# A graph layer on one Trainium2 core: more groups sorted by source, and a first product in one 16-bit pass

## The chip, the cores and the metric

The kernel runs on one core of a Trainium2 chip. Its engines are TensorE (PE, with its weight loads as PEld), VectorE (DVE), ScalarE (ACT), GpSimd (POOL) and SyncE (SP), which mostly issues DMAs. The metric is the device time of one execution in microseconds; times of one kernel agree within about 0.3%.

## What is computed

The reference is one layer of a graph network with residuals, on 6250 nodes of 128 features and 100,000 edges with 4 attributes each. The edges come sorted by their destination. In short:

```python
msg_in = concatenate([x[src], x[dst], edge_attr], axis=1)      # 100000 x 260
h = silu(msg_in @ mW1 + mb1)                                   # 100000 x 128
messages = h @ mW2 + mb2
aggregated = segment_sum(messages, dst, num_segments=6250)
u = silu(concatenate([x, aggregated], axis=1) @ uW1 + ub1)
y = layer_norm(x + (u @ uW2 + ub2), ln_g, ln_b)
out = layernorm(x + y)
```

All inputs and outputs are 32-bit floats. The first product is linear, so it splits into `x[src] @ Wa + x[dst] @ Wb + edge_attr @ We`; the kernel makes two tables, `tab_a = x @ Wa` and `tab_b = x @ Wb + mb1`, once per node.

## The kernel before

Edges are worked through in 98 groups of 1024 (8 tiles of 128). As they are sorted by destination, a group touches few destination nodes: a window of W = 80, which begins at the group's first destination (`base`).

**An unsorted group** (82 of the 98) takes these steps. GpSimd gathers a row of `tab_a` for every edge, with one indirect DMA per tile (`fetch`, L229). SP loads the destinations, broadcast to 80 partitions (`near`, L430), the 80 rows of `tab_b` (`mv`, L584) and the attributes (`st`, L585). VectorE makes two one-hot matrices: `st`, node by edge, with a sum along it that gives the degrees (L593), and `oh`, edge by node (L603). TensorE then multiplies `st` by `mv` (`before_rows`, L618): a 32-bit product per tile with 84 rows, 80 nodes and 4 attributes, into a PSUM buffer `pre`, of which there are two. VectorE adds the gathered rows (L645) and ScalarE applies silu (L646). TensorE sums the result by destination with `oh`, 8 products of 112 columns into the single buffer `pt` (`sums`, L648), and VectorE adds that to `acc`, at an offset in a window of 768 nodes (`add`, L689). The degrees of four groups are transposed and added together (`count`, L679). The first five groups gather rows of `x` instead (`RAW`) and multiply them by Wa on TensorE.

**A sorted group** (16: every fifth from group 15) gathers nothing. Its edges are put in order of their source; then the rows of `tab_a`, which lie in SBUF in three 16-bit parts, are selected by one-hot matrices `O`: per group 168 products of 16 bit into the buffer `po` (`select`, L1051). ScalarE and VectorE make `O` (`picks`, L1016); `Oc` and `at_s` bring the attributes into the new order (`attribute_part`, L1034); `st_s` and `mv_s` give the part of the destinations (L1044). The hidden rows are transposed back (`turned_hidden`, L1072), summed and added as in other groups. These steps are spread over six stages, the group's distance `d` from 5 to 0 (`sorted_before`, `sorted_behind`).

The sort itself is a bitonic network on VectorE (`sort_steps`, L820), over 128 partitions that hold 128 edges each, eight partitions to a group. It runs in steps beside the tables and the first eight groups.

**Order.** The instructions' order on each engine is written by hand (L1179 to 1231). A stage belongs to one unsorted group g: SP loads for the group three stages ahead (`LEAD`), VectorE makes the matrices of the one two ahead, `before_rows` and `hidden` are those of the next, then come the sorted group's parts, then the sums of g and the work on finished nodes (`node_stage`, in batches of 512 nodes). Table b is made batch by batch: two batches ahead of the groups, the others in the stages (`make_b`, L457; `x_stage(k) + 2`). Gathers are paced: every other one waits for a product that a count of TensorE's work chooses (L1242 to 1258). A buffer that is still in use makes the engine wait that would write it, and the queue behind it.

Before all that the tables are built (`tables`, L1136), with the lists of destinations (`lists_1` to `lists_3`). A second way through the kernel, `general`, is only taken for inputs whose destinations are spread too far; it is not taken here.

Of the kernel before, what the change touches and what calls it, by code (L numbers as in the profile page):

```python
# [21 lines left out]
P = 128  # L22
# [5 lines left out]
def kernel(  # L28
# [28 lines left out]
    W = 80  # L57
    WS = 112
    NW = NP + W
    AW = 768  # L60
    K1 = W + ED
# [24 lines left out]
    Q0, QD, QN = 15, 5, 16  # L86
    by_sort = {Q0 + QD * q: q for q in range(QN)}
    listed = [g for g in range(NG) if g not in by_sort]
    R = QN * G
# [6 lines left out]
    assert R % 32 == 0 and W <= S0 and S0 + G * ED == P and listed[RAW] == RAW  # L96
# [10 lines left out]
    def made_for(g):  # L107
        stage = stage_of(g - 4) - 1 if g in by_sort else turn_of(g) - LEAD
        return max(k for k in range(NB) if k < 2 or x_stage(k) + 2 < stage)
# [98 lines left out]
    w_row_i = first.tile([P, W], I32, name="w_row_i")  # L208
    nc.gpsimd.iota(w_row_i, pattern=[[1, W]], base=0, channel_multiplier=0)
# [13 lines left out]
    tab_b = dram.tile([NW, H], F32, name="tab_b")  # L223
    sd = dram.tile([4, QN * GE], F16, name="sd")
    ea_d = dram.tile([ED, NG * GE], F32, name="ea_d")
# [3 lines left out]
    def fetch(g):  # L229
# [20 lines left out]
        ceil_i, pattern=[[BN * P, NB + 1], [0, G]], base=BN * P - W, channel_multiplier=0  # L250
    )
    pos_i = first.tile([R, P], I32, name="pos_i")
    nc.gpsimd.iota(pos_i, pattern=[[P, P]], base=0, channel_multiplier=P * P)
# [8 lines left out]
    if rest:  # L262
        nc.vector.memset(dst_l[low:NG], N)
    nc.sync.dma_start(dst_l[:low], dst[: low * GE].rearrange("(p j) -> p j", j=GE))
# [8 lines left out]
    dst_l = dst_l[:NG]  # L273
    w_row = ps1.tile([P, W], F32, name="w_row")
# [17 lines left out]
    deg_s = []  # L292
    for k in range(3):
        deg_s.append(consts.tile([W, P], F32, name=f"deg_s{k}"))
        nc.vector.memset(deg_s[k], 0.0)

    def deg_at(g):
        s, i = divmod(g - 1, 4) if g else (-1, 0)
        return deg_s[(s + 1) % 3], 32 * i

    def deg_col(g):
        t, c = deg_at(g)
        return t[:, c : c + 1]
# [19 lines left out]
    def lists_1():  # L323
        base_c = first.tile([NG, 1], F32, name="base_c")
        nc.vector.tensor_copy(base_c, dst_l[:, 0:1])
        rel_n = first.tile([P, GE], F32, name="rel_n")[:NG]
        nc.vector.tensor_scalar(rel_n, dst_l, base_c, None, op0=OP.subtract)
        parts.update(base_c=base_c, rel_n=rel_n)
        nc.vector.memset(floor_i[:, 0:1], 0)
        nc.vector.memset(floor_i[:, last[NB - 2] + 1 :], batches[NB - 1][0] * P)  # L330
        nc.vector.memset(ceil_i[:, 84 + G // 2 :], batches[NB - 1][0] * P - W)
# [98 lines left out]
    def destinations(g):  # L430
        near[g] = work.tile([P, GE], I32, name="near")[:W]
        n = min(GE, E - g * GE)
        if n < GE:
            nc.vector.memset(near[g][:, n:], N)
# [1085 lines left out]
```

## Time and profile before

| | |
|---|---|
| median of three runs | 1079.45 us (1077.62 to 1081.79) |
| the profiled execution | 1078.25 us, span of its instructions 1076.5 us |
| mean granted TensorE clock | 0.863 of full speed; in the records it is 1.0 or 0.5 |
| gathers on GpSimd | 614 from `tab_a` (mean 980 ns), 40 from `x` (959 ns) |
| `st` and `oh` on VectorE | 82 at 1261 ns, 82 at 816 ns |
| `O` on ScalarE | 128 at 711 ns and 64 at 1148 ns |
| loads of `near`, `mv`, `st` | 320, 40 and 16 KB per unsorted group |
| DMA | 108.94 MB in 86,890 packets, mean 101 GB/s |

A line of groups reads: line of the kernel, engine, operation, what is written from what, with the shapes, and how often; then the busy time in us and the mean ns of one; then the idle time of the engine just before these instructions, and what ended most of it ("issue" is a wait for nothing that the profile shows). In a timeline the first two numbers are the start and the duration in us of a run of like instructions. The records of TensorE overlap, since products are pipelined: what one costs is read from start to start. A 32-bit product has two records, a 16-bit one has one. In a table of stretches each engine has its busy us and its instructions; PEclk is the granted clock.

### The profile page before, as it was taken

To read this page: it belongs to the slowest core of one execution; us is meant where nothing else is said; L and a number is where in the kernel's file an instruction comes from. 1 tells how busy PE (TensorE), PEld (TensorE's weight loads), DVE (VectorE), ACT (ScalarE), POOL (GpSimd) and SP (SyncE) were. 2 spreads that over 40 slices of the span, in tenths; PEclk is the share of its full clock that TensorE was granted. 3 is DMA by queue.
4 is the path that set the end of the run, shared out by engine and by line. 5 is a ranking of instruction groups with operands and counts; after the bars stand their busy time and mean duration, and the time that the engine had idled before them with its cause. 6 is when DMAs were issued, how large, how long until landed. Compare 5 with 4: busy or idle time off the path is not lost.

```text
span 1076.5 us, 17905 instructions
## 1 busy us (share of the span) xinstructions
PE 807.8 (75%) x6479; PEld 687.8 (64%) x6479; DVE 558.1 (52%) x1357; ACT 404.1 (38%) x543; POOL 641.9 (60%) x665
## 2 busy tenths in 40 slices
PE   5548557668878788877877878777878877877874
PEld 4548455566757576666776666666577666676653
DVE  3463677843555283555373555444374445473282
ACT  1122114533343354344344353343253344363142
POOL 6646557765656666565666566556566566666550
PEclk8778779789888989798998989879879788999795
DMA  9544315342424252525163443424343434242220
GB/s 231 140 114 117 93 57 143 87 101 81 114 85 116 72 137 76 121 75 131 57 152 84 117 109 97 110 80 100 87 112 93 99 92 120 71 111 81 85 77 25
DMA packets 86890, 108.94 MB, mean 101 GB/s; under 512 B 22348, under 2 KB 63456, under 8 KB 86794
## 3 DMA queue, kind: packets, MB, share of 16 engines
q1 hardware_dynamic: 52498, 58.26, 21.3%
q0 software_dynamic: 20928, 42.90, 15.2%
q10 hardware_dynamic: 13368, 6.56, 2.3%
q8 instruction: 53, 0.87, 0.4%
q14 instruction: 43, 0.35, 0.1%
HBM read 96.26 MB, written 11.40 MB: 100 GB/s over the span
## 4 chain that ended last, share of the span: by engine, by line
PE 52%; issue 16%; DVE 13%; another core or an unknown queue 7%; ACT 5%; DMA 3%; POOL 2%; SPq 1%; DVEq 0%; ACTq 0%; POOLq 0%
PE pt L148 14%; PE po L148 14%; PE pre L148 13%; PE pn L148 8%; PE pn L151 2%; POOL ga L234 2%; DMA ga<-tab_a,src_i 1%; DVE st L593 1%; DVE oh L603 1%; ACT h L646 1%; DVE ga L645 1%; ACT O L1027 1%; PE pre L151 1%; DVE O L1023 1%
## 5 line engine op out<-in xcount | busy, mean ns | idle before, releaser
L234 POOL DMA_INDIRECT ga<-tab_a,src_i x614 | 601.9, 980 | 380.4 <-issue 202.4
L148 PE MATMUL pre<-mv,st 128*128 128x128 f32 x1308 | 202.3, 310 | 27.4 <-issue 12.8
L148 PEld LDWEIGHTS pre<-mv,st 128*128 128x128 f32 x1308 | 190.5, 225 | 40.3 <-issue 29.2
L148 PE MATMUL pt<-oh,h 128*128 128x112 f32 x1308 | 191.5, 305 | 25.6 <-issue 12.6
L148 PEld LDWEIGHTS pt<-oh,h 128*128 128x128 f32 x1308 | 180.1, 218 | 39.5 <-issue 24.3
L646 ACT ACTIVATE h<-ga 128x1024 f32<-128x1024 f32 (+1 forms) x78 | 81.1, 1042 | 317.7 <-DVE ga L645 222.6
L692 DVE TENSOR_TENSOR acc<-acc,pt 128x80 f32 x98 | 23.3, 238 | 341.3 <-PE pt L148 104.1
L148 PE MATMUL po<-O,A_low 128*128 128x157 bf16 (+47 forms) x896 | 163.8, 225 | 22.3 <-issue 22.3
L148 PE MATMUL po<-O,A 128*128 128x156 bf16 (+37 forms) x1376 | 140.2, 227 | 36.6 <-issue 33.0
L148 PEld LDWEIGHTS <-A 128*128 128x128 bf16 x1376 | 112.4, 104 | 58.3 <-issue 57.3
L645 DVE TENSOR_TENSOR ga<-ga,pre 128x1024 f32<-128x1024 f32 (+1 forms) x78 | 93.3, 1197 | 54.7 <-PE po L148 22.0
L593 DVE TENSOR_SCALAR_CACHE_REDUCE st<-near,base_p 80x1024 f32<-80x1024 int32 x82 | 103.4, 1261 | 11.9 <-issue 10.4
L148 PEld LDWEIGHTS <-A_low 128*128 128x128 bf16 x896 | 91.0, 103 | 20.6 <-issue 20.3
L1027 ACT ACTIVATE O<-sc,p_less 128x512 bf16<-128x512 f16 x128 | 84.8, 711 | 1.4 <-DMA sc<-sd 1.4
L1028 ACT ACTIVATE O<-O,ones 128x1024 bf16<-128x1024 bf16 x64 | 73.5, 1148 | 2.1
L603 DVE TENSOR_TENSOR oh<-w_row,rel 128x640 f32<-128x640 f32 x82 | 66.9, 816 | 0.8
L151 PE MATMUL pn<-ident,hT 128*128 128x128 f32 x128 | 23.2, 310 | 45.1 <-issue 10.2
L1070 ACT ACTIVATE hT<-po 128x512 f32<-128x512 f32 x32 | 19.0, 593 | 91.4 <-PE po L148 51.7
L234 POOL DMA_INDIRECT ga<-in_x_dram,src_i x40 | 38.3, 959 | 23.2 <-issue 9.9
L151 PEld LDWEIGHTS pn<-ident,hT 128*128 128x128 f32 x128 | 15.5, 154 | 51.1 <-issue 24.3
L148 PE MATMUL pt<-oh,h_s 128*128 128x112 f32 x256 | 34.8, 290 | 12.6 <-ACT h_s L1079 7.9
L148 PE MATMUL pn<-Oc,at_s 128*128 128x512 f32 x64 | 37.8, 675 | 8.0 <-issue 5.6
(221 smaller groups left out, 921.9 us busy)
## 6 DMA issues: line engine op xcount, KB each, us to landing
near<-in_dst_dram SPq DMA_DIRECT2D x81, 320.0 KB
ga<-tab_a,src_i POOLq DMA_INDIRECT x614
sc<-sd SPq DMA_DIRECT2D x16, 512.0 KB
mv<-tab_b SPq DMA_DIRECT2D x82, 40.0 KB
tab_a<-A SPq DMA_DIRECT2D x11, 256.0 KB
tab_b<-o SPq DMA_DIRECT2D x11, 256.0 KB
out_dram<-o ACTq DMA_DIRECT2D x11, 256.0 KB
x<-in_x_dram SPq DMA_DIRECT2D x10, 256.0 KB
```

The lines of the kernel that those rows point to most:

```text
L148: counted(nc.tensor.matmul(to, *operands, **flags), to, share)
L151: counted(nc.tensor.transpose(to, *operands), to)
L234: ins = nc.gpsimd.indirect_dma_start(out=rows[g][:, i, :], out_offset=None, in_=x if g < RAW else tab_a[:, :], in_offset=bass.IndirectOffs ...
L593: nc.vector.tensor_scalar(stbuf[turn_of(g) % NST][:W], near.pop(g), base_p[:W, g : g + 1], 0.0, op0=OP.is_equal, op1=OP.add, accum_out=deg ...
L603: nc.vector.tensor_tensor(oh[g][:, :n, :W], w_row[:, None, :].to_broadcast([P, n, W]), rel[:, g, :n, None].to_broadcast([P, n, W]), op=OP. ...
L645: nc.vector.tensor_add(s[:, i], s[:, i], p[:, i])
L646: nc.scalar.activation(h[:, i], s[:, i], AF.Silu)
L692: nc.vector.tensor_add(to, to, pt[:, :W])
L1023: nc.vector.tensor_scalar(O[:, j], key, p_rows[:, r : r + 1], None, op0=OP.is_equal)
L1027: nc.scalar.activation(O[:, j], key, AF.Square, bias=p_less[:, r : r + 1])
L1028: nc.scalar.activation(O[:, 2:], O[:, 2:], AF.Relu, bias=ones[:, 0:1], scale=-1.0)
L1070: nc.scalar.activation(now["hT", half], now.pop("po"), AF.Silu)
```

## The change

Two things change together, and several follow from them.

1. **More sorted groups.** Every fourth group from 15 on is sorted, 20 instead of 16. In the sort 80 partitions hold 256 edges each, four to a group.
2. **The first product in one 16-bit pass.** The table b and We are split into three 16-bit parts each (high, middle, low), the attributes too. The product of a tile has 126 rows: 3 parts x 30 nodes, and 9 pairs of parts x 4 attributes. The 30 nodes move with the tile: tile i of a group begins 8 i nodes behind the group's base. The base is a multiple of 8, and a new margin F = 16 lies ahead of table b and the sums.

What follows: the split table is kept in DRAM by eighths (`tab_p`), and a group's `mv` takes four DMAs; `near` comes from a stored 16-bit table of offsets (`off_d`), 90 partitions of 2 KB; the attributes come as 36 rows of 2 KB. `st` is one comparison of 16-bit values without a sum. `oh` has 32 columns per tile, padded to 112. The sums go to overlapping columns of `pt`, so the buffer is first cleared by a product with zeros, and the degrees are made by four products with ones. A group's window has W = 88 nodes. The splits of table b and of the attributes are made in steps spread over a stage (`b_steps`, `attribute_steps`), in a `pre` buffer.

The diff, cut to its core:

```diff
+    S = 8
+    V, VS, VW = 30, 32, 112
+    W = S * (G - 1) + VS
+    F = 2 * S
+    KB, K1 = 3 * V, 3 * V + 9 * ED
-    Q0, QD, QN = 15, 5, 16
+    Q0, QD, QN = 15, 4, 20
+    GR = 4
+    C = GE // GR
...
     def destinations(g):
-        near[g] = work.tile([P, GE], I32, name="near")[:W]
...
-            dst[g * GE : g * GE + n].rearrange("(o e) -> o e", o=1).to_broadcast([W, n]),
+        near[g] = work.tile([P, GE], F16, name="near")[:KB]
+        nc.sync.dma_start(near[g], off_d[g : g + 1, :].to_broadcast([KB, GE]))
...
+    def attribute_steps(c, pm):
...
+        def high():
+            nc.scalar.copy(v, ea_l.pop(c).rearrange("q (j d) -> q d j", d=ED))
+            nc.scalar.copy(t[:, 0], v)
+
+        def middle():
+            nc.vector.tensor_sub(v, v, t[:, 0])
+            nc.scalar.copy(t[:, 1], v)
+
+        def low():
+            nc.vector.tensor_sub(t[:, 2], v, t[:, 1])
+            nc.scalar.dma_start(
...
+    def b_steps(k, pm):
...
+        def high():
+            nc.vector.tensor_add(v, v, b1[:m, None, :].to_broadcast([m, BN, H]))
+            nc.scalar.copy(t[:, :, 0], v)
+            tb = node.tile([P, BN, H], F32, name="o")[:m]
+            nc.scalar.copy(tb, v)
...
+        def middle():
+            nc.vector.tensor_sub(v, v, t[:, :, 0])
+            nc.scalar.copy(t[:, :, 1], v)
+
+        def low():
+            nc.vector.tensor_sub(t[:, :, 2], v, t[:, :, 1])
...
-        nc.sync.dma_start(mv[turn_of(g) % NM][:W], tab_b[bass.ds(bases[g], W), :])
-        nc.sync.dma_start(stbuf[turn_of(g) % NST][W:K1], ea_d[:, g * GE : (g + 1) * GE])
+        to = mv[turn_of(g) % NM].rearrange("r i f -> r (i f)")
+        for a in range(D - G + 1):
+            n = min(S, V - a * S)
+            nc.sync.dma_start(
+                to[3 * S * a : 3 * S * a + 3 * n],
+                tab_p[:n, :, bass.ds(bases[g] + a, G), :].rearrange("b s d f -> (b s) (d f)"),
+            )
+        cols = slice(g * GE, (g + 1) * GE)
+        nc.sync.dma_start(
+            stbuf[turn_of(g) % NST][KB:K1],
+            ea_d[:, cols].rearrange("(o r) e -> o r e", o=1).to_broadcast([3, 3 * ED, GE]),
+        )
...
         nc.vector.tensor_scalar(
-            stbuf[turn_of(g) % NST][:W],
-            near.pop(g),
-            base_p[:W, g : g + 1],
-            0.0,
-            op0=OP.is_equal,
-            op1=OP.add,
-            accum_out=deg_col(g),
+            stbuf[turn_of(g) % NST][:KB], near.pop(g), third[:KB], None, op0=OP.is_equal
         )
...
             matmul(
-                pre[g][:, i, :], st[:, i, :], mv[turn_of(g) % NM], start=True, stop=not raw
+                pre[g][:, i, :], st[:K1, i, :], mv[turn_of(g) % NM][:K1, i, :],
+                start=True, stop=not raw, share=1 / 4,
             )
...
+    def cleared(pt):
+        matmul(pt, none[:, : pt.shape[0]], none, start=True, stop=False, share=1 / 4)
+
+    def degrees(g, pt):
+        to = pt[0:1, WP : WP + W]
+        if g in by_sort:
+            transpose(to, deg_s[by_sort[g] % 2], ident[:W, :W])
+            return to
+        for a in range(D - G + 1):
+            matmul(
+                to[:, a * S : (a + G) * S], ones[:, 0:1], oh[g][:, :, a * S : (a + 1) * S],
...
+            cleared(pt)
+            if g < NG - 1:
+                degrees(g, pt)
+            for i in range(n):
+                matmul(
+                    pt[:, i * S : i * S + VW], h[:, i, :], oh[g][:, i, :],
+                    start=False, stop=i == n - 1,
+                )
...
+        chain = []
+        for k in range(2, NB):
+            if j == x_stage(k) + 2:
+                chain = b_steps(k, wide()[:, :BN])
         for c in range(1, NC):
-            at = stage_of(max(1, c * EC // GE - 9))
+            at = stage_of(max(1, c * EC // GE - 10))
...
+                chain = [None] + attribute_steps(c, wide().rearrange("p i f -> p (i f)"))
+        chain = iter(chain)
+
+        def go_on():
+            step = next(chain, None)
+            if step:
+                step()
```

`go_on` is called four times in a stage: at its start, after the matrices, after the silu of the next group, and after the sums.

## The prediction

> **What bounds the kernel now.** I read the page's first part and the busy times by stretch, then the groups, the chain of waits, and the timelines of TensorE and GpSimd.
>
> ```profile
> PE 807.8 (75%) x6479; PEld 687.8 (64%) x6479; DVE 558.1 (52%) x1357; ACT 404.1 (38%) x543; POOL 641.9 (60%) x665
> ```
> ```profile
> core 0: us, PE busy (x) PEld busy (x) DVE busy (x) ACT busy (x) POOL busy (x), PEclk, DMA share, GB/s
> 0.00:89.00 89.00, 51.88 (x288) 46.93 (x289) 37.74 (x131) 17.16 (x23) 53.23 (x65) 0.79 0.60 157
> 89.00:239.00 150.00, 101.87 (x738) 90.18 (x736) 100.05 (x253) 47.18 (x52) 97.03 (x92) 0.82 0.37 99
> 239.00:1039.00 800.00, 632.16 (x5357) 534.59 (x5358) 405.23 (x918) 325.57 (x443) 486.02 (x503) 0.89 0.39 99
> 1039.00:1076.00 37.00, 21.86 (x102) 16.06 (x100) 15.05 (x55) 14.17 (x26) 5.65 (x6) 0.68 0.11 31
> ```
>
> The stretch 239 to 1039 is the steady part. TensorE is busy 79% of it. GpSimd's 503 gathers look like 61%, but its timeline shows the real load:
>
> ```profile
> 454.74 0.95 POOL L234 DMA_INDIRECT ga<-tab_a,src_i  x1 [0.49 <-issue]
> 455.99 0.95 POOL L234 DMA_INDIRECT ga<-tab_a,src_i  x1 [0.30 <-issue]
> 457.25 0.94 POOL L234 DMA_INDIRECT ga<-tab_a,src_i  x1 [0.31 <-issue]
> ```
>
> A gather costs 1.25 us from start to start, 10.0 us for a group of 8; 503 of them fill 629 of 800 us, also 79%. The two are level, and tied both ways: gathers are paced by products, and a group's products need its gathered rows. VectorE (51%) and ScalarE (41%) have room. The chain through this stretch is mostly TensorE ("po" 18.1%, "pt" 15.9%, "pre" 11.8%, "pn" 10.3%) and "issue" 17.4%; 9.6% of it, 77 us, is an unknown queue (5.2%), gathers (2.6%) and their landing (1.8%). So TensorE binds, and gathers bind in places. The groups show the holes:
>
> ```profile
> L148 PE MATMUL pre<-mv,st 128*128 128x128 f32 x1308 | 202.3, 310 | 27.4 <-issue 12.8
> L148 PEld LDWEIGHTS pre<-mv,st 128*128 128x128 f32 x1308 | 190.5, 225 | 40.3 <-issue 29.2
> L148 PEld LDWEIGHTS <-A 128*128 128x128 bf16 x1376 | 112.4, 104 | 58.3 <-issue 57.3
> ```
>
> The last column is idle time with no visible cause: 57.3 us before 1376 16-bit loads, about 42 ns each.
>
> **The change, part by part.** Busy means overlap, so TensorE is costed from start to start, at full clock:
>
> ```profile
> 307.55 1.95 PE L148 MATMUL pre<-mv,st 128*128 128x128 f32 x16
> 309.33 1.02 PE L148 MATMUL po<-st_s,mv_s 128*128 128x512 f32 x2
> ```
> ```profile
> 326.73 0.27 PE L148 MATMUL po<-O,A 128*128 128x130 bf16 x2
> 326.84 0.22 PE L148 MATMUL po<-O,A_low 128*128 128x130 bf16 x1
> 326.90 0.28 PE L148 MATMUL po<-O,A 128*128 128x125 bf16 x2
> ```
>
> Sixteen 32-bit records of "pre" (two per product) take 1.78 us, 0.222 per product. Two 16-bit products of 130 columns take 0.11 us, 0.055 each.
>
> *First product.* 654 products by 0.222 (145.2 us) become 622 by 0.055 (34.2): -111.0 us. Here I weigh the Trainium skill, "TensorE: Matmul & The Clock Gate", section "Back-to-back issue gap": it puts a sustained 128-column load-and-multiply pair at about 81 ns. By it the term is 622 x 0.026 = 16 us less good, which would cancel the whole TensorE gain below. The row is the same pair on this chip; I take 0.055.
>
> *Degrees.* VectorE no longer sums them; each unsorted group gets a clearing product of 256 columns (16-bit; by the row, 256/130 x 0.055 = 0.11) and four 32-bit products of 64 columns with one stationary column. Half of "pre" is 0.056 per record; two records, four products: 0.45. Over 78 groups +44 us, less 26 transposes (-4), plus 20 for sorted groups (+2). The four may run as low as the load allows (0.2 us) or as high as a 128-column product (0.9): 25 to 79 us.
>
> *Four more sorted groups.* Beyond the sums that every group has, one costs TensorE about 9 us of selection (168 products at a mean of some 0.054 in the timeline), four records of "pn<-Oc" (0.435 each, 1.74), four of "po<-st_s" (0.43, 1.72) and 8 transposes (0.115, 0.9): 13.4 us, times 4 = +53.5.
>
> TensorE's sum: -111 + 44 - 2 + 53.5 = -15.5, divided by the page's mean granted clock 0.863: **-18 us**. In steady groups it is no gain: with sums of 1.8 us per group and 3.5 us of node work per five groups, five before take 4 x 3.6 + 15.2 + 3.5 = 33 us at full clock (6.6 each), four after 3 x 2.85 + 15.2 + 2.8 = 26.6 (6.6 each). Freed time is respent on sorting.
>
> *Gathers.* 32 fewer, 32 x 1.25 = 40 us of GpSimd. Per group the floor falls from 8.0 to 7.5 us; in a cycle of three unsorted groups and a sorted one it is 30 us, against about 40 that TensorE with its holes needs (before 40 of 51). Of the 77 us that gathers hold on the chain I let 30 go: that is between 0, if those waits are the landing latency that stays, and 60. **-30 us.** What is late next there is TensorE.
>
> *VectorE.* Per unsorted group L593 (1261 ns plus 78 for the read) becomes a 16-bit comparison without sum: twice the row "O<-sc" 128x512 bf16 (0.36), so 0.65; L603 goes from 640 to 256 elements, 0.82 to 0.42. Saved 1.1 us x 78 = 86. Added: two subtractions per batch of table b (13 x 1.4), as many per attribute chunk (10 x 1.2), four sorted groups (4 x 7, rows L1005 to L1085). It lies beside TensorE; I count 0. The sort has 104 compare operations of 128 elements where it had 98 of 64 at about 0.2 us; at 0.27 to 0.30 it is 8 to 11 us longer. It runs between groups 0 and 8 and was on the chain at 141 to 147 us; these groups save 8 x 1.1 on the same engine. Sum 0. Without that cover, +10.
>
> *ScalarE.* +12.6 us per sorted group (8 x 0.711, 4 x 1.148, hT and h_s 4 x 0.58) = +50, and three copies of 0.6 per batch: 404 becomes about 490, 46%. Hidden.
>
> *The chains of splits.* Table b and the attribute chunks are now split in four steps through one stage, in one of the two "pre" buffers. The last subtraction (0.69 us, as L462) stands on VectorE behind acc (0.24) and deg (0.23) of the same stage; the next stage's first product waits for that buffer, and behind it on TensorE the sorted products and the sums. So up to 1.4 us in 20 stages: 0 to 28, where node products stand between it is covered; I take **+8**.
>
> *Tables.* Steps written inline make VectorE wait for ScalarE: for two batches 2.7 us each, for chunk 0 about 2. The stretch to 69 us has VectorE idle 57%, but TensorE waits for its copies (L468). SP gets 23 more small DMAs (filling we_d, off_d and tab_p; 0.3 to 0.4 us each) and holds behind them tab_a's writes. 0 to 16; **+8**.
>
> *Queues in the steady part.* SP issues 6 DMAs for an unsorted group instead of 3 (four for mv), some 25 per cycle at 0.3 to 0.45: 10 of 40 us. A write of tab_p waits for loads of mv under way, and later loads for it (L463 did so 7 times, 19.6 us); behind it stand near, mv and st, with a lead of two stages, 20 us. Moved per group: (3 x 432 + 800) / 4 = 524 KB against 459, gathers 384 against 410: +4% at a DMA share of 0.39. Nothing charged. The skill speaks against one load: "DMA: Bandwidth & Descriptors", section "Rules for kernel authors", says that a leading dimension of c under 16 confines a DMA to c engines. The attribute load now leads with 3: 72 KB on 3 engines, 24 KB each, about 0.9 us at the page's 27 GiB/s, against 4 KB on 4. The trace has no such transfer; with three stages of lead I take 0, and by the rule, if gathers wait for those three engines, 78 x 0.9 = 70 us of their time is at stake, little of it on the chain.
>
> *Issue holes.* Hardware instructions on TensorE, counted in both built programs (four per 32-bit product, two per 16-bit), rise from 12,960 to 14,520. If holes go with time, 0. If with pairs, 672 more selections by about 36 ns (98 us over 2688 in the three groups of A) are +24, the first product -7, the degrees +14: +31. I take **+6**, nearer to time, since the holes come in clusters and not evenly.
>
> Sum: -18 - 30 + 8 + 8 + 6 = -26 on the profiled execution's 1078.25 us (span 1076.5): 1052. The median of the runs is 1.2 higher, 1079.45: **1053.5 us**.
>
> **The rivals.** *Holes go with instructions (slower).* TensorE is the only bound, gathers give back nothing, and the issue holes before 16-bit loads grow with the denser stream: -18 + 8 + 8 + 31 = +29, 1108 us. For it: per steady group TensorE's work is not smaller. Against it: 77 us of gathers on the chain. It decides as soon as the holes cost more than what the gathers give back, about 30 us.
>
> *Gathers were the bound.* Then the 40 us and half of what else they hold go: -60 with -18 and +16: 1017 us. For it: 79% forced load. Against it: TensorE rarely waits for gathered rows directly.
>
> *Give and take.* Relief, holes and chains cancel: 1079, within 5 us. That the change does not do what it says is excluded: the built program has one 16-bit pass per tile and 20 sorted groups.
>
> **How the numbers follow.** Forecast 40% (own range 1028 to 1073), gathers 12%, cancelling 8%, holes 40% (1085 to 1125). A measurement of this kernel tells 0.5% (5.4 us) from no change. Faster 0.50, same 0.09, slower 0.41. As both signs hold weight, the range spans them: 1012 to 1115.
>
> **What would show it.** "pre" as 16-bit with one record per tile, 8 of them in about 0.45 us; degrees near 0.45 us a group; 622 gathers at the same 1.25 us; the unknown and gather shares of the steady chain falling from 77 us to under 50; "issue" idle before 16-bit loads near 42 ns each (if it grows, the slower rival holds). TensorE waiting for a VectorE subtraction before "pre" for more than 1.4 us a time would show the chains mis-sized. The forecast is wrong if a cycle of four groups takes over 41 us between 239 and the last sorted group.

## The result, and the profile after

The changed kernel takes 1109.95 us, the median of four runs (1107.92 to 1115.91). The kernel before, run on the same chip, takes 1080.62 us (1077.62 to 1083.15). The ratio is 1.028 with an interval of 1.023 to 1.033: the change makes the kernel slower by 29 us. The profiled execution took 1110.15 us, its span is 1108.4 us, and the mean granted clock is 0.847 (before 0.863). Executions of one kernel differ by more than the 0.3% given above: by 0.7% here, and by up to 2.2% in the runs below.

These are the busy times of the engines, and then the table by stretch, with the same bounds as before except for the end.

```profile
PE 845.2 (76%) x7234; PEld 685.3 (62%) x7234; DVE 509.8 (46%) x1370; ACT 474.2 (43%) x662; POOL 618.9 (56%) x635
```
```profile
0.00:89.00 89.00, 44.93 (x207) 39.71 (x208) 37.44 (x128) 18.34 (x28) 45.42 (x59) 0.90 0.59 153
89.00:239.00 150.00, 101.68 (x736) 82.88 (x736) 91.90 (x250) 53.40 (x63) 96.62 (x93) 0.75 0.44 118
239.00:1039.00 800.00, 652.33 (x5971) 528.20 (x5970) 351.09 (x892) 378.56 (x533) 453.01 (x460) 0.86 0.42 106
1039.00:1108.00 69.00, 46.28 (x323) 34.49 (x322) 29.41 (x101) 23.92 (x39) 23.84 (x25) 0.79 0.22 59
```

In the steady stretch TensorE is busier than before (652 us for 632), its clock is lower (0.86 for 0.89), and GpSimd does 460 operations in place of 503. VectorE has lost 54 us and ScalarE has gained 53. The groups and the timeline of TensorE show the parts of the change:

```profile
L245 POOL DMA_INDIRECT ga<-tab_a,src_i x582 | 578.7, 994 | 427.4 <-issue 197.9
L158 PEld LDWEIGHTS <-A 128*128 128x128 bf16 x1720 | 145.2, 107 | 89.4 <-issue 89.0
L158 PE MATMUL pre<-mv,st 126*128 126x128 bf16 x622 | 68.1, 254 | 25.5 <-issue 16.5
L158 PE MATMUL pt<-oh,ones 128*1 128x64 f32 x616 | 52.2, 230 | 8.0 <-issue 7.8
```
```profile
628.76 0.28 PE L158 MATMUL pt<-none 1*128 1x256 bf16 x1
628.97 0.61 PE L158 MATMUL pt<-oh,ones 128*1 128x64 f32 x8
629.51 1.70 PE L158 MATMUL pt<-oh,h 128*128 128x112 f32 x13
```
```profile
622.34 0.61 PE L158 MATMUL pre<-mv,st 126*128 126x128 bf16 x8
622.79 0.20 PE L158 MATMUL po<-O,A 128*128 128x19 bf16 x2
```

The first product is one 16-bit record per tile: eight of them take 0.45 us from start to start (622.34 to 622.79), 0.056 each. From start to start the clearing product costs 0.21 us (628.76 to 628.97) and the degrees of a group 0.54 us (628.97 to 629.51).

**Where the time came from.** VectorE adds every group's sums to `acc`, and the start of that addition dates the group. These are group 0's additions, first of the kernel before, then after:

```profile
89.34 0.24 DVE L692 TENSOR_TENSOR acc<-acc,pt 128x80 f32 x1 [10.41 <-PE pt L148]
```
```profile
103.53 0.24 DVE L814 TENSOR_TENSOR acc<-acc,pt 128x88 f32 x1 [6.77 <-PE pre L158]
```

So 14.2 us are lost before group 0. From group 0 to 20 the changed kernel gains 4.9 us (209.3 for 214.2). From group 20 to 92 it takes 747.2 us in place of 722.7: 24.5 us are lost, and a cycle of four groups takes 41.5 us, over the 41 us that the prediction named as its sign of being wrong. The last groups and the end give 2 us back. Together that is 31.9 us, the difference of the spans.

**What TensorE's time consists of.** I took its timeline between 239 and 1039 us apart. A run of like products is charged from its start to the next start, less the idle time in between; what of it lies in stretches of half clock is halved, and the other half is called clock. By the groups whose addition to `acc` falls in the stretch, in us per group:

| kernel | work at full clock | clock | idle | sum | issue idle in 100 us | gathers in 100 us |
|---|---|---|---|---|---|---|
| before | 6.93 | 0.99 | 2.04 | 9.96 | 11.6 | 62.9 |
| after | 7.27 | 1.22 | 1.90 | 10.39 | 8.6 | 57.4 |

"Issue idle" is the part of TensorE's idle time that ends with no cause that the profile shows. So the work rose by 0.34, the lower clock cost 0.23, and the idle time fell by 0.14. The work can be relied on; the other two are no larger than what single profiles of equal steady parts differ by (the table of the next section has e_iota and e_start, which change only the start: 7.32 and 7.31 of work, but 1.04 and 1.00 of clock, where after has 1.22). By the same count, from before to after: first product 1.49 to 0.37, degrees and clearing 0 to 0.59, selection 1.85 to 2.37, the other sorted parts (`pn<-Oc`, `po<-st_s`, `pn<-ident,hT`) 0.86 to 1.18.

### The profile page after: what moved, and what is told of

Same layout as the page of the kernel before. It is cut to its first block, busy times and chain, and to the rows that moved or that the text cites. A ratio compares the mean times of both kernels' runs of the same rounds, so it can differ in the third digit from the quotient of the medians.

```text
span 1108.4 us, 20413 instructions
## 1 busy us (share of the span) xinstructions
PE 845.2 (76%) x7234; PEld 685.3 (62%) x7234; DVE 509.8 (46%) x1370; ACT 474.2 (43%) x662; POOL 618.9 (56%) x635
## 2 busy tenths in 40 slices
DMA packets 115693, 120.04 MB, mean 108 GB/s; under 512 B 50083, under 2 KB 79355, under 8 KB 115583
## 4 chain that ended last, share of the span: by engine, by line
PE 49%; issue 11%; DVE 11%; ACT 8%; another core or an unknown queue 3%; DMA 3%; SPq 1%; ACTq 1%; DVEq 0%; POOL 0%; POOLq 0%
PE pt L158 18%; PE po L158 17%; PE pn L158 7%; PE pre L158 4%; ACT O L1167 2%; DMA ar<-sd 2%; PE pn L161 2%; ACT O L1168 2%; DVE ga L747 1%; DVE st_s L1179 1%; DVE y L871 1%; ACT h L748 1%; ACT o L884 1%; DVE O L1163 1%
## 5 line engine op out<-in xcount | busy, mean ns | idle before, releaser
L158 PE MATMUL po<-O,A 128*128 128x147 bf16 (+37 forms) x1720 | 179.5, 232 | 70.1 <-ACT O L1168 33.2
L158 PE MATMUL po<-O,A_low 128*128 128x144 bf16 (+25 forms) x1120 | 211.5, 230 | 10.7 <-issue 10.5
L158 PEld LDWEIGHTS <-A 128*128 128x128 bf16 x1720 | 145.2, 107 | 89.4 <-issue 89.0
L748 ACT ACTIVATE h<-ga 128x1024 f32<-128x1024 f32 (+1 forms) x74 | 76.7, 1039 | 111.7 <-DMA ga<-tab_a,src_i 48.6
L158 PEld LDWEIGHTS <-A_low 128*128 128x128 bf16 x1120 | 117.3, 106 | 11.2 <-issue 11.2
L158 PE MATMUL pre<-mv,st 126*128 126x128 bf16 x622 | 68.1, 254 | 25.5 <-issue 16.5
L158 PEld LDWEIGHTS <-st 126*128 126x128 bf16 x622 | 54.9, 118 | 34.0 <-issue 30.9
L158 PE MATMUL pt<-oh,ones 128*1 128x64 f32 x616 | 52.2, 230 | 8.0 <-issue 7.8
L158 PE MATMUL pre<-w,xT 128*128 128x128 f32 (+2 forms) x186 | 44.8, 410 | 16.8 <-ACT xT L490 9.1
L158 PE MATMUL pt<-oh_s,h_s 128*128 128x88 f32 x320 | 54.2, 341 | 0.0
L158 PE MATMUL po<-O,A_high 128*128 128x51 bf16 (+12 forms) x520 | 49.0, 223 | 6.7 <-issue 6.3
```

Source lines behind the costliest of these rows:

```text
L158: counted(nc.tensor.matmul(to, *operands, **flags), to, share)
L748: nc.scalar.activation(h[:, i], s[:, i], AF.Silu)
```

## The experiments

Eighteen kernels ran. Ratios are to the kernel before on the same chip, whose median lay between 1069 and 1072 us in these runs; the changed kernel's own ratio is 1.028. The last three columns are those of the table above (for e_half up to 958 us, where its sorted groups end, for e_free and b_free the first up to 1400 and 1150; a dash stands where a trace was not taken apart). One profile stands behind each row. From group 20 to 92, e_iota and e_start take 732.5 and 734.3 us where after takes 747.1, with the same steady part, on chips on which the kernel before is 1% faster; so a difference of 0.2 us per group in clock or idle says little.

| run | median, us | ratio | clock | work, clock, idle | issue idle | gathers |
|---|---|---|---|---|---|---|
| e_16: 16 sorted groups | 1113.3 | 1.041 [1.034, 1.048] | 0.834 | 6.81, 1.21, 2.40 | 13.2 | 61.5 |
| e_13: 13 sorted | 1143.1 | 1.067 [1.059, 1.074] | 0.803 | 6.44, 1.63, 2.89 | 14.8 | 61.3 |
| e_10: 10 sorted | 1145.1 | 1.071 [1.065, 1.077] | 0.784 | 5.81, 1.58, 3.45 | 14.0 | 64.8 |
| e_iota: lists earlier | 1104.4 | 1.033 [1.027, 1.038] | 0.852 | 7.32, 1.04, 1.93 | 6.5 | 58.5 |
| e_start: lists and We earlier | 1096.0 | 1.027 [1.023, 1.030] | 0.856 | 7.31, 1.00, 1.95 | 8.3 | 58.2 |
| e_rep3: first product three times | 1110.4 | 1.030 [1.018, 1.042] | 0.889 | 8.07, 0.72, 1.74 | 7.2 | 57.8 |
| e16_rep4: e_16, four times | 1135.9 | 1.061 [1.052, 1.070] | 0.873 | 7.82, 0.95, 1.89 | 11.5 | 59.8 |
| b_16bit: before, 16-bit product | 1057.4 | 0.991 [0.986, 0.996] | 0.827 | 5.87, 1.33, 2.68 | 12.8 | 62.7 |
| e_nodeg: no degrees | 1093.3 | 1.024 [1.020, 1.028] | 0.817 | 6.83, 1.28, 2.02 | 8.4 | 59.0 |
| e_pick4: O on VectorE | 1100.9 | 1.029 [1.025, 1.033] | 0.841 | 7.33, 1.17, 1.73 | 8.8 | 58.6 |
| e_lead: gathers further ahead | 1108.5 | 1.039 [1.028, 1.050] | 0.849 | 7.37, 1.07, 1.95 | 7.5 | 58.5 |
| e16_lead: e_16, the same | 1120.1 | 1.045 [1.036, 1.054] | 0.811 | 6.65, 1.42, 2.31 | 10.7 | 61.4 |
| e_free: gathers not paced | 1476.6 | 1.374 [1.364, 1.384] | 0.744 | 7.49, 2.55, 4.81 | 16.2 | 42.8 |
| e16_free: e_16, not paced | 1351.7 | 1.257 [1.247, 1.266] | 0.759 | – | – | – |
| b_free: before, not paced | 1267.0 | 1.184 [1.173, 1.194] | 0.802 | 7.11, 1.56, 3.47 | 19.5 | 53.2 |
| b16_free: b_16bit, not paced | 1274.1 | 1.183 [1.174, 1.193] | 0.751 | – | – | – |
| e_half: half of the gathers | 1016.8 | 0.949 [0.946, 0.952] | 0.877 | 7.16, 0.67, 1.39 | 0.5 | 33.2 |
| e16_nochain: e_16, no chains | 1129.4 | 1.052 [1.047, 1.056] | 0.822 | 6.72, 1.49, 2.46 | 9.9 | 60.0 |

**First: the number of sorted groups, and the start.** The edits of e_16, e_13 and e_10 differ in two numbers:

```diff
-    Q0, QD, QN = 15, 4, 20
+    Q0, QD, QN = 15, 5, 16
```

For e_13 they are 6 and 13, for e_10 they are 8 and 10. e_iota moves the two lists ahead of the first gathers in GpSimd's order:

```diff
+    w_row_i = first.tile([P, G * VS + W], I32, name="w_row_i")
+    nc.gpsimd.iota(
+        w_row_i[:, : G * VS], pattern=[[S, G], [1, VS]], base=0, channel_multiplier=0
+    )
...
     p_row_i = first.tile([P, G], I32, name="p_row_i")
```

Expected of e_16:

> The changed kernel with 16 sorted groups, every fifth (QD = 5, QN = 16), as before the change; the single 16-bit pass and everything else stay. Theory A (TensorE sets the steady part, and a sorted group costs it more than the gathers it frees are worth): at full clock a cycle of five is 4 x 3.05 + 15.2 + 3.5 = 30.9 us, 6.2 per group against 6.8 now; before and after, a steady group takes 1.52 times its full-clock work (10.04 from 6.6, 10.38 from 6.8), so 9.4 us per group: 70 us less than after, about 1040. Rival B (gathers hold the stages; fewer of them is a gain): 32 gathers more at 1.25 us, 40 us longer, about 1150. Rival C (what costs is the machinery of the single pass, its DMAs, chains and degrees): within 10 us of after, about 1105.

Of e_13:

> The changed kernel with 13 sorted groups, every sixth. Theory A: 5 x 3.05 + 15.2 + 4.2 = 34.7 us at full clock in a cycle of six, 5.8 per group, 8.8 us with the same factor; the gathers' floor is 8 x 1.25 x 5/6 = 8.3 us per group, near it, so part of the gain is lost: 1020 to 1045. Rival B: 56 gathers more, about 1180. Rival C: about 1100.

Of e_10:

> The changed kernel with 10 sorted groups, every eighth. Theory A: TensorE would need 5.4 us per group at full clock, 8.2 with the factor, but the gathers' floor is 8.75 us: the gathers now bind and the time turns up again, equal to or above the run with 13, 1030 to 1070. If the time goes on falling, gathers can run closer to their floor than I think. Rival B: about 1200.

Theory A falls. Fewer sorted groups are slower, though TensorE's work per group falls from 7.27 to 6.81, 6.44 and 5.81 us. Idle time and the clock take the place of the work: idle rises from 1.90 to 3.45, and the granted clock falls from 0.847 to 0.784. The four more sorted groups alone (e_16 to after) are worth 1.3% by the ratios, 14 us; their intervals nearly touch, and the profiled steady stretches of the two are alike (10.4 us per group), so it is 14 us at most. Rival C, the machinery of the single pass, comes nearest for e_16. Rival B, the gathers, had the direction right in all three steps and the size wrong: by the ratios they cost 14, 27 and 5 us, where it said 40, 30 and 20.

Expected of e_iota:

> The changed kernel with the index lists w_row_i and third_i made on GpSimd ahead of the first eight gathers, where the kernel before had w_row_i. Theory D (VectorE stands 9.6 us at the start behind GpSimd's queue, and TensorE's first products behind VectorE): 10 us shorter, about 1100. Rival: the tables wait next for SP's loads and writes of We, so only 0 to 4 us come back.

In the changed kernel VectorE had stood still for the list, where it did not before (the kernel before is first):

```profile
5.75 0.22 DVE L276 CAST w_row<-w_row_i 128x80 f32<-128x80 int32 x1
```
```profile
15.64 0.52 DVE L297 CAST w_row<-w_row_i 128x344 f32<-128x344 int32 x1 [9.58 <-issue]
```

With the list moved, the next thing was late. This is from VectorE's timeline of e_iota:

```profile
23.13 0.21 DVE L582 CAST we_t<-we 4x128 bf16<-4x128 f32 x1 [12.14 <-DMA we<-in_L_gnn_mW_dram]
```

SP issues the load of We, 2 KB, only at 17.17 us, behind its loads of x and of the lists and the first write of `tab_a`, and VectorE waits 12.1 us for it with everything behind it. Group 0's addition stays at 102.3 us. The rival holds.

**Second: is TensorE's work the limit?** e_rep3 issues each first product three times, e16_rep4 four times:

```diff
-            matmul(
+            for again in range(1 if raw else 3):
+                matmul(
```

> The changed kernel with each tile's first product issued three times instead of once (from group 5 on); the later ones overwrite the first with the same values. It adds 2 x 8 x 0.055 = 0.9 us of TensorE work at full clock to each of 73 unsorted groups, 64 us. Theory A (TensorE's work sets the time): 64 / 0.85 = 75 us longer, about 1185. Theory E (TensorE is short of work in the stages without sorted parts, where the gathers set the pace; its clock falls to half there and the next stage is run slowly, so that saved work comes back as a slower clock): most of the repeats lie in idle time and keep the clock up; the granted clock rises from 0.847 to over 0.87 and the time stays within +5 to +35 us of after.

> The run with 16 sorted groups (1113 us, ratio 1.041 to the kernel before, clock 0.834) with each first product issued four times: +1.3 us of TensorE work per group at full clock, 77 groups, 102 us in all, which brings TensorE's work for the first product back to what the 32-bit products took. Theory A: 102 / 0.85 = 120 us longer, ratio about 1.15. Theory E: the clock rises to over 0.86 and the ratio is within 0.02 of 1.041.

The stretch 239 to 1039 of e_rep3:

```profile
239.00:1039.00 800.00, 666.53 (x6939) 550.22 (x6938) 350.98 (x887) 382.30 (x539) 461.02 (x463) 0.92 0.43 106
```

There are 968 more products in the same 800 us, about as many gathers, and the clock is 0.92 in place of 0.86. The 64 us of added work cost nothing that the runs can tell (the interval is wide, some -12 to +15 us). In e16_rep4 102 us cost about 21, give or take 12. TensorE's work, one for one, is not what sets the time, and a part of it is paid by the clock, which rises with the added work. e_lead and e16_lead gave the gathers one stage more:

```diff
-    AHEAD = 4
+    AHEAD = 5
-    PACE = 3.5
+    PACE = 4.5
-    NM = 4
+    NM = 3
-            "hT": lambda: pool.tile([P, HB], F32, name="hT", bufs=2),
+            "hT": lambda: pool.tile([P, HB], F32, name="hT"),
```

> The changed kernel with gathers one stage further ahead (AHEAD 5 for 4, seven buffers for six, PACE 4.5 for 3.5); to make room mv has three buffers for four and hT one for two, which nothing should wait for. Theory E (in the stages without sorted parts TensorE waits for what gathers bring; in the sorted stage of 21 us GpSimd stands still behind products): GpSimd gathers on through the sorted stage, and 10 to 35 us come back, 1075 to 1100. Theory A (TensorE's work sets the steady part): within 5 us of after, ratio 1.023 to 1.033.

> The same lead for gathers with 16 sorted groups. Theory E: it gains more than with 20, since more gathers are to be made beside the sorted stage: from 1.041 to between 0.98 and 1.01 of the kernel before. Theory A or C: ratio within 0.01 of 1.041.

Neither can be told from its base; the intervals overlap. In e_lead's trace group 0 comes 11.9 us later than in after (115.4 us), and the groups 20 to 92 take 730.7 us where after's take 747.1; but e_iota, with no longer lead, takes 732.5. So nothing speaks for that part of theory E, that a longer lead of the gathers would help, and a gain of a few us is not excluded.

**Third: the parts of the change by themselves.** b_16bit is the kernel before with nothing but the product changed:

```diff
-        st = stbuf[turn_of(g) % NST].rearrange("k (i c) -> k i c", i=G)
+        st = stbuf[turn_of(g) % NST].bitcast(BF16).rearrange("k (i c s) -> k i c s", i=G, s=2)
+        m = mv[turn_of(g) % NM].bitcast(BF16).rearrange("k (f s) -> k f s", s=2)
...
-                pre[g][:, i, :], st[:, i, :], mv[turn_of(g) % NM], start=True, stop=not raw
+                pre[g][:, i, :], st[:, i, :, 1], m[:, :, 1],
+                start=True, stop=not raw, share=1 / 4,
```

> The kernel before, with the first product read from the upper 16 bits of the 32-bit tiles (it leaves out the lower bits of table b and of the attributes): one 16-bit pass per tile with 84 rows, and nothing else of the change, no degrees on TensorE, no split chains, the same loads. TensorE's work falls by 1.1 us per group, 107 us in all. Theory A (TensorE's work sets the time): about 90 us shorter, 985. Theory E (a saving of TensorE's work comes back mostly as half clock and idle, as three products for one cost nothing): 0 to 35 us shorter, with the granted clock down from 0.863 to about 0.83.

```profile
239.00:1039.00 800.00, 582.35 (x4890) 472.20 (x4891) 409.48 (x945) 329.63 (x451) 481.83 (x502) 0.84 0.40 99
```

TensorE's work per group falls by 1.06 us, as large as predicted, and the time by 0.9%, 10 us. Of the 1.06 us 0.34 went to a lower clock and 0.64 to idle time; the 502 operations of GpSimd in 800 us are those of before (503). This is the clearest run of the study: a saving of 107 us on the busiest engine was worth a tenth of itself (4 to 15 us by the interval).

e_nodeg leaves out the degree products:

```diff
-        for a in range(D - G + 1):
+        for a in range(D - G + 1 if g == NG - 1 else 0):
```

> The changed kernel without the four products with ones that make the degrees (they are left out except in the last group; the cleared row is added instead). TensorE's work falls by 0.44 us per group, 34 us. Theory A: 34 / 0.85 = 40 us shorter, about 1070. Theory E: 0 to 12 us shorter, and the granted clock at or under 0.847.

It gained some 4 us for 34 us of work, which the intervals can't tell from nothing, and its clock fell to 0.817: theory E again, and not the 40 us of theory A. e_pick4 makes O on VectorE alone:

```diff
-            if j < 2:
+            if j < 4:
...
-        nc.scalar.activation(O[:, 2:], O[:, 2:], AF.Relu, bias=ones[:, 0:1], scale=-1.0)
```

> The changed kernel with all of the one-hot rows O made on VectorE (four comparisons of about 0.36 us per step) and none on ScalarE: ScalarE loses 80 x 2.5 = 200 us, VectorE gains 80 x 0.72 = 58 us. Theory F (in the stage before a sorted group ScalarE's queue holds two picks, square roots, table loads and the outputs, and TensorE waits for O: 33 us, and for what follows): 15 to 40 us shorter. If ScalarE's queue is not what is late: within 5 us; if VectorE's queue is the tighter one: longer.

No difference in time. TensorE then waits for O for 27.5 us, all on VectorE, in place of 43.0 (33.2 on ScalarE, 9.8 on VectorE), and longer for `st_s` ahead of the transposes (17.3 for 11.5) and in issue holes ahead of `pn` (10.6 for 3.7). e_start adds to e_iota that We is loaded ahead of the other batches of x:

```diff
     nc.scalar.dma_start(w1, mW1[: 2 * H].rearrange("(s k) f -> k s f", k=P))
+    we = first.tile([ED, H], F32, name="we")
+    nc.sync.dma_start(we, mW1[2 * H :])
```

> The changed kernel with w_row_i and third_i made ahead of the first gathers and We loaded ahead of the other batches of x (with the lists alone, VectorE waited 12 us for We's load instead, and group 0 stayed where it was). Theory D (VectorE, held at the start, is what delays the tables): group 0's sums come at 90 to 95 us instead of 103, and the whole is 8 to 13 us shorter. Rival (SP's queue, with nine writes of we_d and four loads of mv per group, sets group 0): group 0 at 99 to 103, 0 to 4 us shorter.

Group 0 comes at 97.8 us and group 14 at 245.3 (253.2 in after), so 6 to 8 us of the start come back in the trace; the ratio, 1.027 for 1.028, can't tell that from nothing. The theory is half right: of the 14.2 us before group 0, 5.7 come back and 8.5 are not placed.

**Fourth: the gathers.** e_free, e16_free, b_free and b16_free leave the gathers of the steady part to run as soon as a buffer is free:

```diff
-            if (g > RAW or g < RAW and G * g + i > 2) and i % 2 == 0:
+            if g < RAW and G * g + i > 2 and i % 2 == 0:
```

> The changed kernel with the gathers of the steady part not tied to products (no paced gathers from group 5 on; only a free buffer holds them). Theory G (the pacing lets one group of eight gathers go per unsorted stage; in a stage without sorted work they need 8 x 1.25 = 10 us, so these stages take 9.4 to 11 us however little TensorE has to do, and beside the sorted stage of 21 us GpSimd stands still): GpSimd gathers on in the sorted stage, the short stages shrink to what TensorE needs, about 8 us, and a cycle goes from 42 to 37 or 38 us: 40 to 80 us shorter, 1030 to 1070. If something else holds the short stages: within 10 us of after (ratio 1.02 to 1.035). If gathers that crowd hurt the other loads: longer.

> 16 sorted groups (ratio 1.041) with the gathers not tied to products. Theory G: it gains more than with 20, since four of five groups are gathered: ratio 0.95 to 1.00. Otherwise within 0.01 of 1.041.

> The kernel before with the gathers of the steady part not tied to products. Theory G: the pacing holds the kernel before too (short stages of 10.5 to 12.4 us), but its TensorE work fills them better: 10 to 40 us shorter, ratio 0.96 to 0.99. Otherwise 0.99 to 1.02.

> The kernel before with the first product read from the upper 16 bits (it leaves out the lower bits, ratio 0.991 with pacing) and gathers not tied to products. Theory G: what kept the 107 us of saved TensorE work from showing was the gathers' pace per stage, so now 40 to 80 us come: ratio 0.92 to 0.96. If the cause lies elsewhere: 0.98 to 1.00.

All four are slower than the kernel before, by 18 to 37%. Their gathers go mostly in bursts of 8 to 16. In e_free's trace, between 300 and 1100 us, TensorE's issue idle is 25% of the time in which gathers run and 5% of the rest; in the paced kernel after it is 8% and 10%. Of the 4.5 us per group that e_free has more than after, about 1.5 are issue idle, 1.3 the clock, and most of the rest other waits. So gathers in bursts go with more holes on TensorE, and the pacing is no mere loss. Theory G, as I had put it, falls.

e_half keeps the pacing and leaves out every other tile's gather:

```diff
-        for i in range(tiles_of(g)):
+        for i in range(0, tiles_of(g), 2 if 20 <= g < NG - 2 else 1):
```

> The changed kernel with every other tile's gather left out between groups 20 and 95 (the rows of those tiles are what an earlier group left there; six fixed buffers in place of rotating ones), 228 gathers fewer; the paced ones are kept, so the pacing stays. A group then needs 5 us of GpSimd in place of 10. If the gathers, by their number, hold the short stages (theory G'): these fall from 9.4 to 11 us to what TensorE needs, 7 to 8, and 40 to 80 us come, ratio 0.95 to 0.99. If the stages are held by the chain of TensorE, VectorE and ScalarE itself: within 12 us of after, ratio 1.015 to 1.03.

It is 7.7% faster than after, some 84 us for 228 gathers. But the short stages hardly moved (9.45 to 8.67 us, and 11.14 to 11.19), against theory G'. The stage with the sorted sums did: 21.4 to 16.9 us. The waits of TensorE between 239 and 958 us show what went. Columns are the engine and line that wait, for whom, us in total, times, the longest. First the kernel after, then e_half; of each its longest wait for O and all its issue holes:

```profile
PE po L158 <- ACT O L1168: 31.8, 16, 2.9
PE po L158 <- issue: 31.8, 47, 2.8
PE pt L158 <- issue: 11.4, 18, 1.1
PE pre L158 <- issue: 9.5, 11, 2.2
PE pn L161 <- issue: 4.1, 6, 0.9
PE pn L158 <- issue: 3.7, 5, 0.9
```
```profile
PE po L158 <- ACT O L1172: 52.0, 22, 2.9
PE pre L158 <- issue: 3.5, 6, 1.1
PE po L158 <- issue: 0.2, 1, 0.2
```

The holes without a visible cause are gone: 60 us become 4, before "po" 31.8 us become 0.2. The instructions of TensorE per group are the same. TensorE's wait for O, 31.8 us in after, is 52.0 now and is next. With the gaps much of the half clock went, and the same 719 us hold more products (after first):

```profile
239.00:958.00 719.00, 583.46 (x5346) 472.38 (x5346) 315.70 (x797) 341.80 (x482) 404.43 (x411) 0.86 0.43 107
```
```profile
239.00:958.00 719.00, 611.08 (x6095) 502.52 (x6095) 356.43 (x909) 379.89 (x537) 233.23 (x240) 0.92 0.40 98
```

e_half changes two things at once: there are fewer gathers, and they hardly follow each other any more. In after most of them go in rows of two (93 times between 239 and 1039 us) and of four (54 times), in e_half 201 of 218 rows up to 958 us are a single gather. A row is taken to go on while the next gather starts within 1.6 us. The traces show that the second goes with the holes. For each moment I took the place in its row of the last gather that started within the 3 us before, and the share of such moments that lies in issue holes:

| kernel | no gather | first | second | third | fourth | later |
|---|---|---|---|---|---|---|
| before | 0.0% | 0.5% | 2.7% | 8.5% | 17.9% | 32.6% |
| after | 0.6% | 2.5% | 4.5% | 9.1% | 26.1% | 15.5% |
| e_free, 300 to 1100 us | 0.9% | 2.1% | 3.0% | 6.0% | 24.3% | 35.7% |
| e_half, to 958 us | 1.7% | 0.3% | 0.0% | – | – | – |

So the holes come late in a row: 76 of the 93 us of them in before, and 42 of 68 in after, lie behind a fourth or later gather. Beside a single gather there are hardly more than beside none. That also explains why in after the time in which gathers run looked no worse than the rest. Here is such a place in after, the first and the last gather of a row of four, and TensorE, whose row of 16 like products breaks up behind the last:

```profile
572.67 0.95 POOL L245 DMA_INDIRECT ga<-tab_a,src_i  x1 [0.30 <-issue]
576.43 0.97 POOL L245 DMA_INDIRECT ga<-tab_a,src_i  x1 [0.30 <-issue]
```
```profile
574.97 1.59 PE L158 MATMUL pt<-oh,h 128*128 128x112 f32 x12
576.97 0.26 PE L158 MATMUL pt<-oh,h 128*128 128x112 f32 x1 [0.41 <-issue]
577.70 0.26 PE L158 MATMUL pt<-oh,h 128*128 128x112 f32 x1 [0.47 <-issue]
```

This is a reading of traces; no run changed the length of the rows and nothing else.

**Fifth: the split chains.** e16_nochain makes table b and the attributes in one step each:

```diff
-                chain = b_steps(k, wide()[:, :BN])
+                b_whole(k)
...
+    def b_whole(k):
...
+        nc.vector.tensor_add(tb, pm[:m], b1[:m, None, :].to_broadcast([m, BN, H]))
...
+        for s in range(3):
+            nc.scalar.copy(t[:, :, s], tb)
```

> 16 sorted groups with the single pass (ratio 1.041), and table b and the attributes in the stages no longer split in steps: one addition into SBUF, three copies of the same values on ScalarE (the middle and low parts are left out: they hold the high part again), made at once in the buffer pn; no subtractions, no hold on a pre buffer. Between the kernel before with a 16-bit product alone (0.991) and this one's base (1.041) lie 53 us; degrees are known to be worth about 5 of them and the start up to 17. Theory H (the split chains tie ScalarE and VectorE to each other and hold pre in 20 stages, which costs the rest): ratio 1.01 to 1.025. If the chains are hidden, as I took them nearly to be: 1.033 to 1.045.

It is no faster than e_16, if anything slower (1.052 for 1.041; the intervals just touch). Making the splits at once gains nothing, so theory H falls. What the same copies cost at once is not told apart from what the chains in steps cost.

## Why the prediction was wrong

**The step that failed** is TensorE's sum, above all its first term. The prediction said "So TensorE binds, and gathers bind in places" and turned TensorE's work into time one for one: the -111 us of the first product, divided by the clock 0.863, stand for -129 us. b_16bit makes this saving by itself, and 10 us come. Three more runs give the rate at which this kernel turns TensorE's work into time: about 21 us for 102 (e16_rep4), some 4 for 34 (e_nodeg), nothing that can be told for 64 (e_rep3). The rate lies between 0 and 0.2, with intervals that reach 0.3. The rest goes into idle time and into the granted clock, which the sum held fixed at 0.863. Everything that was added to make the saving possible stood against some 10 us, not against 129.

The same sum in three parts shows what the other terms did:

| part | predicted, us | by the runs, us |
|---|---|---|
| the 16-bit product alone (b_16bit) | -129 | -10 (ratio 0.991) |
| what makes it exact: degrees 49, chains, tables and holes 22 (b_16bit to e_16) | +71 | +54 (0.991 to 1.041) |
| four more sorted groups: TensorE 62, gathers -30 (e_16 to after) | +32 | at most -14 (1.041 to 1.028) |
| sum | -26 | about +30 |

The first part was 119 us too good. The other two were too dear by some 63 us together, and that the forecast missed by no more than 56 us is luck.

**The clock is a term of its own.** In the trace before, the clock changes after multiples of 3.41 us, and it is 1.0 or 0.5. Cut into stretches of that length between 239 and 1039 us, a stretch at full clock in which TensorE was busy under half was followed by half clock in 27 of 31 cases, and one busy over 80% by full clock in 100 of 100. From half clock it came back in 30 of 36 cases after a stretch busy over 90%, and in 4 of 16 after a lesser one. After is alike (15 of 17; 101 of 101; 38 of 42 and 2 of 22). Between 50 and 80% at full clock the two differ: 6 of 52 were followed by half clock before, 24 of 53 after. The Trainium skill, "TensorE: Matmul & The Clock Gate", part 1 on the clock gate, states such a free-running window of about 3.4 us with two rates; the trace agrees. By these counts a long gap is paid twice, and work that fills a gap can be partly free. That bears on this case: e_rep3's clock is 0.92 in the steady stretch and its work the highest of all.

**The size of the work.** The prediction had steady groups of equal work; they grew by 0.34 us at full clock. The first product fell by 1.12 us a group, near the -111 us / 98 of the prediction: the row of 0.055 us was right (0.056 in after), and the rule of about 81 ns for a pair, which the prediction set aside, does not hold here. The degrees and the clearing cost 0.59 in place of 0.45 (0.54 and 0.21 us per unsorted group). The sorted parts listed above grew by 0.84.

**Gathers, -30.** The mechanism was partly right, and its place was not. The pitch of gathers stayed at 1.25 us (median). The signal that I named held too: on the steady chain the unknown queue is 4.8% of 800 us, 38 us, and gathers with their landing are 9 us by the trace, 47 in all where it was 77. These 30 us left the chain as forecast, and the time did not fall. But "what is late next" was not only TensorE: it was `ar<-sd` (2.0%) and O (5.4%), with the lower clock. Where gathers are seen to cost is in TensorE's holes, behind rows of three and more. Per gather left out, e_half gained 0.37 us; the four more sorted groups gained at most 14 us for 32 gathers, their selection paid.

**Issue holes, +6.** They fell, from 11.6 to 8.6 us in 100. Neither of the two answers, "with time" or "with pairs", was right: they go with the gathers, and among these with the later ones of a row. From 33 gathers in 100 us to 57 to 59, 60 to 63 and 65, the paced kernels show 0.5, 6.5 to 8.8, 9.9 to 14.8, and 14.0 us of holes. And the row that I read them from, idle before 16-bit loads, was no measure: for `<-A` it is 89.0 us in after, 52 ns a load, which by the prediction's own sign spoke for the slower rival; and it is still 81.4 in e_half, where TensorE's multiplications have almost no holes.

**Tables, +8.** Measured 14.2 us. I had looked for VectorE's waits for ScalarE; the list `w_row_i` had moved past GpSimd's queue of eight gathers, which the diff shows, and VectorE stood 9.6 us behind it. That is a move past a queue that was left out of the sum. It was not the whole: without it group 0 comes 1.3 us earlier (e_iota), and with the load of We moved as well 5.7 us (e_start).

**Chains, +8, and queues of VectorE and ScalarE, 0.** No wait of TensorE for a subtraction ahead of "pre" shows, and making the splits at once gained nothing. ScalarE's 0 was not the whole truth: TensorE waits 33.2 us for O made there, where before it was 4.7; but e_pick4 shows that without that wait others take its place.

**The rivals.** "Holes go with instructions" gave 1108 us, and 1110 came, but by luck and not for its reason: holes fell. "Gathers were the bound" had the better mechanism and the wrong sum, since it counted the saving of TensorE as well and nothing for the rest of the single pass.

**What stays open.** Of the 54 us some 17 lie before group 0 (85.7 us in b_16bit, 102.6 in e_16) and 7 more before group 14. The rest, 0.51 us per steady group, is not placed. TensorE's work is 0.94 us per group higher in e_16 than in b_16bit, 0.6 of it degrees and clearing; at the rate of e16_rep4 that is some 0.2 us. Making the splits at once gained nothing; the more numerous loads of SP (50,083 packets under 512 B for 22,348 before), and among them the attributes' load that leads with 3, which the prediction put at 0, were not tried by themselves. How a row of gathers makes a hole on TensorE is open too, and so is whether rows of at most two would be faster.

No exact version that beats the kernel before came out of this.

## What to carry to other kernels

Before a saving on the busiest engine is counted as time, add the same amount of useless work there and look whether the kernel becomes slower; here three products for one were nearly free, and the saving of the same size was nearly worthless. Take the granted clock as a result of the schedule, not as a constant to divide by: work, half clock and idle time are three terms that trade against each other. When an engine has holes without a visible cause, lay them beside the other engines' work by its place in a row, and not only by its rate. And list, for every added step, what it moves past on each queue, in the start-up as well.

## What the hardware showed

- TensorE's holes of some 0.7 us, which end with no cause in the profile, lie mostly behind the later gathers of a row on GpSimd: they take 0.5 to 2.5% of the time behind a first gather, 6 to 9% behind a third and 18 to 26% behind a fourth (before, after, e_free). With mostly single gathers (e_half) 60 us of them become 4 in 719 us, with the same products per group.
- Leaving the gathers unpaced, so that they go in bursts of mostly 8 to 16 at 1.25 us, cost 18% (before) and 34% (after, 1.374 over 1.028).
- The single clearing product of 256 columns takes 0.21 us up to the start of the 32-bit product behind it, where two 16-bit products of 130 columns among their like took 0.11 us. Whether its neighbours are the reason was not tried.
